# Seams between the phases of a four-layer scan network: an add moved into the Mamba passes, a norm interleaved with convolutions, weights loaded beside other phases

## The chip, the core and the metric

The kernel runs on one core of one Trainium2 chip. The metric is the device time of one execution in microseconds (us). Three executions of the kernel before gave 20165.96, 20166.1 and 20180.66 us, so its median is 20166.1 us.

## The reference

Four images of 48 x 48 positions and 192 channels (2304 tokens each) pass through four layers. Everything is float32. Cut to what matters here:

```python
# layer 0: two bidirectional Mamba blocks with a norm and a residual between them
def bimamba(u, i):              # P[i], P[i+1]: weights of the two directions
    return mamba(u, P[i]) + mamba(u[:, ::-1], P[i + 1])
...                             # first block on the columns of x (tokens w-major);
...                             # layernorm of its output, turned to rows, plus x: "mixed";
...                             # second block on "mixed": x1
# mamba(u): xz = u @ in.T; causal conv of 3 taps, silu; B, C, delta by projections;
#   h[t] = exp(delta[t] * A) * h[t-1] + delta[t] * u[t] * B[t];  y[t] = sum_n h[t] * C[t]
#   (y + xc * D) * silu(z) @ out.T            (384 inner channels, 16 states)
# layer 1 (VSS block), xl, xr = the two channel halves of x1
y = relu(bn2(conv3x3(bn1(xl), conv1))); y = relu(bn3(conv3x3(y, conv2)))
xl_out = relu(conv1x1(y, conv3))
xi, z = split(layernorm(xr) @ in_proj.T)      # 192 channels each
xi = silu(depthwise_conv3x3(xi))              # then four directional scans of xi,
...                                           # norm, gate silu(z), out projection, + x1
# layer 2 (SS2D): four directional scans, norm.  layer 3: row and column Mambas, MLP
```

Note that the two Mamba outputs of a block are added position by position. The kernel's second pass of a block runs its tokens backwards and writes its output in mirrored order (`mirror`), so both passes' outputs have the same layout in HBM.

## The kernel before, in words

**Phases.** `network` calls one function after the other: `mamba_pair` for weights 0 and 1 (0 to 3147 us of the profiled execution), `mix_images` (to 3330), `mamba_pair` for weights 2 and 3 (to 6483), `vss_inputs` (to 6997), `scan_layers` (layers 1 and 2, to 13478), `row_mambas` (to 19711) and `mlp`. The phases hand images to each other through HBM. Each opens its own pools of SBUF memory, so a tile of a later phase may have to wait until the tile of an earlier one whose memory it takes is free.

**Orders.** Each engine's instructions are kept in the order in which the program writes them: PE (matmuls), DVE (VectorE), ACT (ScalarE, `k.act`, `k.copy`), POOL (GpSimd, `k.g`), and SP, which issues all the DMAs (`nc.sync.dma_start`). An instruction that waits therefore holds back everything behind it on its engine. A tile pool with `bufs=n` gives out n buffers per tag; the next tile of that tag waits until the oldest is free.

**The scan.** A pass over an image is six `MambaJob`s of 384 tokens (`CH`), 48 jobs in a pair of passes over four images. A job has 12 groups: 3 blocks of 128 channels by 4 groups of 4 states. `run_jobs` walks over all groups. For each group DVE forms `inputs` (delta, u and the broadcast B, `bcb`) and runs the scan `h`; ACT forms the decays `a` two groups ahead; POOL copies the last state and multiplies `h` by C (`weigh`); PE sums over the states into `y` (`reduce`), one group behind. Once per block POOL also forms `dus` (delta times u, `drive`) and the gated `yt` (`gate`). The rest of a job's work (projections, convolution, gates, and the output projection of the job before) is given out as *units* with slots: a unit `((start, end), ...)` has its matmuls begun in one of the 12 groups and its result taken by ACT in another. The output projection of a job is made in slots 4 and 6 of the next job: two matmul units for the channel halves (`Q` = 96 each), taken to the tile `o` by ACT; with the second, SP stores `o` (288 KB). For B and C, SP issues four broadcasts (`bcb<-bc`) per job.

**The mix.** Before, the two passes of a pair write two image lists, `oa[0]` and `oa[1]`. `mix_images` loads for each image both outputs (`s0`, `s1`, 1728 KB each) and the residual `res`; POOL adds `s1` to `s0`, chunk by chunk (`both`, L903); then six norm stages follow, software-pipelined over 24 chunks: mean on PE, center on DVE (L173), square on ACT and its mean on PE, variance on DVE (L190), root on ACT, scale on DVE (L201), affine on ACT and DVE (L216). After an image's last chunk, `post` adds the turned result to `res`, one channel half on DVE and one on POOL (L907), and SP stores the image (`mixed`). Only then does the next `mamba_pair` load its weights (L796 to L870), derive `A` (ACT exp, DVE) and `diag` (DVE), and load the first `u`.

**The VSS inputs.** For each image `load` reads the two outputs of the second pair (`ob`), POOL adds them (L981), and the sum is stored as `x1`. `norm` normalizes the right channel half to `xn`. Per image the order is: the batch norm of the left half into the padded tile `pads[0]` (ACT), the projection of `xn` to two padded tiles (PE, ACT), 18 depthwise taps on DVE (L1026, L1030: 2 x 9 over a 96 x 2304 tile), the load of the next image, the first 3x3 convolution (PE, nine matmuls per chunk), the norm of the next image, the projection of `z` (PE, ACT), silu of `vxi` (ACT), its turned copy (POOL, L1057) and stores, then the second 3x3 convolution and the 1x1 convolution (PE, ACT) and the store of `xl`.

**The scan layers.** `scan_layers` first loads the weights of layers 1 and 2: per layer and direction `xpT`, `dtT` twice and `vec` (class `Weights`, L796 to L806), with `A` derived on ACT and DVE (L814), and `dsum` and `ddiag` on DVE; then the scan jobs of layer 1 begin by loading `xs` from the images `xi_hw` and `xi_wh`.

Of the kernel before, what the change touches and what calls it, by code (L numbers as in the profile page):

```python
# [17 lines left out]
B = 4  # L18
# [474 lines left out]
class MambaJob(ScanJob):  # L493
# [3 lines left out]

    skips = True

    def __init__(self, k, pools, w, c0, rev, prev, src, dst, mirror=False, twin=None):  # L500
        super().__init__(k, pools, w, c0, rev, prev)
        self.src, self.dst, self.mirror, self.twin = src, dst, mirror, twin
        self.paired = False
        if twin is not None:
            twin.paired = True
# [35 lines left out]
    def units(self, last):  # L541
# [41 lines left out]
        if self.twin is not None:  # L583
            self.z = self.twin.z
            outputs = last.outputs((7, 7), (9, 9)) if last is not None else []
            bc, deltas = self.projections(lambda: self.xs, (3, 3), (5, 5))
            return [conv(0, 0, 0), conv(1, 1, 2), conv(2, 2, 2), bc, *deltas, *outputs]
        outputs = last.outputs((4, 4), (6, 6)) if last is not None else []
# [8 lines left out]
            *outputs[1:],  # L597
            *deltas,
            gate(0, 9, 10),
# [17 lines left out]
    def outputs(self, *slots):  # L617
# [4 lines left out]
        jobs = [self] if self.twin is None else [self.twin, self]  # L622

        def project(m, slots):
            def act(ps):
                if m == 0:
                    self.o = k.tile(self.pools.one, [Q, 2, CH], "o")
                k.copy(self.o[:, m, ::step], ps)
                if m == 1:
                    d0 = L - CH - self.c0 if self.mirror else self.c0  # L630
                    k.nc.sync.dma_start(halves(self.dst)[:, :, d0 : d0 + CH], self.o)
# [15 lines left out]
        return [project(m, slots[m]) for m in range(2)]  # L647
# [65 lines left out]
def run_jobs(jobs, side=None):  # L713
# [29 lines left out]
    for t in range(len(groups) + gated):  # L743
# [8 lines left out]
        if at == taken + 3 and n + 1 == len(jobs) and n:  # L752
            Stream(jobs[n - 1].outputs((0, 0), (0, 0))).run(per)
# [28 lines left out]
    Stream(jobs[-1].outputs((0, 0), (0, 0))).run(per)  # L782
# [3 lines left out]
class Weights:  # L786


    def __init__(self, k, pool, wide, rank, xpT, dtT, vec, tag):
# [22 lines left out]
        self.A = k.tile(pool, [128, 3, n], f"A{tag}")  # L812
        k.act(self.A, self.vec[:, :, 1 : 1 + n], AF.Exp)
        nc.vector.tensor_scalar(self.A, self.A, -1.0, None, ALU.mult)  # L814


class MambaWeights(Weights):
    def __init__(self, k, pool, inT, xpT, dtT, vec, tag):
        super().__init__(k, pool, 128, 12, xpT, dtT, vec, tag)
        nc = k.nc  # L820
# [22 lines left out]
def mamba_pass(k, pools, w, rev, src, dst, mirror=False):  # L843
    jobs = []
    for n in range(NCH):
        c0 = (NCH - 1 - n if rev else n) * CH
        prev = jobs[-1] if jobs else None
        jobs.append(MambaJob(k, pools, w, c0, rev, prev, src, dst, mirror))
    return jobs
# [12 lines left out]
def mamba_pair(k, weights, srcs, outs, mirror):  # L862

    with ExitStack() as ctx:
        pool = ctx.enter_context(k.tc.tile_pool(name="w", bufs=1))
        ws = []
        for n, (inT, xpT, dtT, vec, outT) in enumerate(weights):
            w = MambaWeights(k, pool, inT, xpT, dtT, vec, f"_{n}")
            w.outT = k.tile(pool, [128, 3, C], f"outT_{n}")
            k.nc.sync.dma_start(w.outT, outT.rearrange("(k p) m -> p k m", p=128))  # L870
            ws.append(w)
        pools = ScanPools(k, ctx, 1, False)
        jobs = []
        for b in range(B):
            for n in range(2):
                jobs += mamba_pass(k, pools, ws[n], n == 1, srcs[b], outs[n][b], mirror and n == 1)
# [3 lines left out]
def mix_images(k, o, hw, norm, out_hw):  # L880


    nc, tc = k.nc, k.tc
    with (
# [5 lines left out]
        nc.sync.dma_start(nw, norm.rearrange("(k p) v -> p k v", p=Q))  # L890
        s0, s1, res = {}, {}, {}

        def pre(b):
            s0[b] = k.tile(pool, [Q, 2, L], "s0")
            nc.sync.dma_start(s0[b], halves(o[0][b]))
            s1[b] = k.tile(pool, [Q, 2, L], "s1")
            nc.sync.dma_start(s1[b], halves(o[1][b]))
# [3 lines left out]
        def both(b, c):  # L901
            at = slice(c * CH, (c + 1) * CH)
            nc.gpsimd.tensor_tensor(s0[b][:, :, at], s0[b][:, :, at], s1[b][:, :, at], ALU.add)  # L903

        def post(b):
# [7 lines left out]
            nc.sync.dma_start(halves(out_hw[b]), res[b])  # L913
# [7 lines left out]
        pipelined([both, *stages], pre, post)  # L921


def vss_inputs(k, o, bn, vec, conv1, conv2, conv3, inT, x1, xl, xi_hw, xi_wh, zs):
# [4 lines left out]
    with (  # L929
# [19 lines left out]
        w1 = k.tile(one, [Q, 9, Q], "w1")  # L949
        nc.sync.dma_start(w1, conv1.rearrange("t i o -> i t o"))  # L950
        w2 = k.tile(one, [Q, 9, Q], "w2")
        nc.sync.dma_start(w2, conv2.rearrange("t i o -> i t o"))
        w3 = k.tile(one, [Q, Q], "w3")
        nc.sync.dma_start(w3, conv3)
        win = k.tile(one, [Q, 4 * Q], "win")
        nc.sync.dma_start(win, inT)
        v = k.tile(one, [Q, 2, 10], "v")
        nc.sync.dma_start(v, vec.rearrange("(k p) v -> p k v", p=Q))
# [15 lines left out]
        x, xn = {}, {}  # L974

        def load(b):
            x[b] = k.tile(pool, [Q, 2, L], "vx")
            nc.sync.dma_start(x[b], halves(o[0][b]))
            x2 = k.tile(one, [Q, 2, L], "vx2")
            nc.sync.dma_start(x2, halves(o[1][b]))  # L980
            nc.gpsimd.tensor_tensor(x[b], x[b], x2, ALU.add)  # L981
            nc.sync.dma_start(halves(x1[b]), x[b])
            xn[b] = k.tile(pool, [Q, 1, L], "xn")

        def norm(b):
            stages = norm_stages(
# [10 lines left out]
            for t in range(NCH + len(stages) - 1):  # L997
# [4 lines left out]
        load(0)  # L1002
        norm(0)
        for b in range(B):
# [6 lines left out]
            )  # L1011
            for c in range(NCH):
                for e in range(2):
                    p, shaped = ps()
                    k.mm(
                        p, [(win[:, e * Q : (e + 1) * Q], xn[b][:, 0, c * CH : (c + 1) * CH])]
                    )
                    k.copy(inside(pads[2 + e], c), shaped)

            xi = k.tile(one, [Q, 2, L], "vxi")  # L1020
            for i in range(2):
                acc = square(xi[:, i, :])
                for t in range(9):
                    taps = pads[2 + i][:, t // 3 : t // 3 + S, t % 3 : t % 3 + S]
                    if t == 0:
                        nc.vector.tensor_scalar(  # L1026
                            acc, taps, v[:, i, 1:2], v[:, i, 0:1], ALU.mult, ALU.add
                        )
                    else:
                        nc.vector.scalar_tensor_tensor(  # L1030
                            acc, taps, v[:, i, 1 + t : 2 + t], acc, ALU.mult, ALU.add
                        )
            if b + 1 < B:
                load(b + 1)
            xlt = k.tile(one, [Q, L], "xlt")
            for c in range(NCH):
                _, shaped = ps()
                k.mm(shaped, [(w1[:, t, :], window(pads[0], c, t)) for t in range(9)])
                k.act(
                    inside(pads[1], c), shaped, AF.Relu, scale=scale[:, 1:2], bias=shift[:, 1:2]  # L1040
                )
            if b + 1 < B:
                norm(b + 1)
            z = k.tile(one, [Q, 2, L], "vz")
            for c in range(NCH):
                at = slice(c * CH, (c + 1) * CH)
                for e in range(2):
                    p, _ = ps()
                    k.mm(p, [(win[:, (2 + e) * Q : (3 + e) * Q], xn[b][:, 0, at])])
                    k.act(z[:, e, at], p, AF.Silu)  # L1050
            nc.sync.dma_start(halves(zs[b]), z)
            for i in range(2):
                k.act(xi[:, i, :], xi[:, i, :], AF.Silu)
            nc.sync.dma_start(halves(xi_hw[b]), xi)
            xiT = k.tile(one, [Q, 2, L], "vxiT")
            for i in range(2):
                nc.gpsimd.tensor_copy(square(xiT[:, i, :]), flipped(xi[:, i, :]))  # L1057
            nc.sync.dma_start(halves(xi_wh[b]), xiT)
            last = None
            for c in range(NCH + 1):  # L1060
                y = None
                if c < NCH:
                    p, shaped = ps()
                    k.mm(shaped, [(w2[:, t, :], window(pads[1], c, t)) for t in range(9)])
                    y = k.tile(pool, [Q, CH], "vy")
                    k.act(y, p, AF.Relu, scale=scale[:, 2:3], bias=shift[:, 2:3])
                if last is not None:
                    p, _ = ps()
                    k.mm(p, [(w3, last)])
                    k.act(xlt[:, (c - 1) * CH : c * CH], p, AF.Relu, bias=b3)  # L1070
                last = y
            nc.sync.dma_start(xl[b], xlt)
# [90 lines left out]
def scan_layers(k, layers, ends):  # L1163
# [3 lines left out]
    with ExitStack() as ctx:  # L1167
        nc = k.nc
        pool = ctx.enter_context(k.tc.tile_pool(name="w", bufs=1))
# [7 lines left out]
        for n, (xpT, dtT, vec, rank, post, src) in enumerate(layers):  # L1177
            ws = [
                Weights(k, pool, 64, rank, xpT[i], dtT[i], vec[i], f"_{n}{i}") for i in range(4)
            ]  # L1180

            ds = k.tile(pool, [64, 3, 6], f"ds{n}")
            nc.sync.dma_start(ds, post.rearrange("(k p) v -> p k v", p=64))
            dsum = k.tile(pool, [64, 3], f"dsum{n}")
# [458 lines left out]
```

## Time and profile before

| | |
|---|---|
| median of 3 executions | 20166.1 us |
| profiled execution, its own time | 20169.74 us |
| span of the profile | 20168.0 us, mean PE clock 0.933 |
| busy: PE, DVE, ACT, POOL | 87%, 90%, 63%, 73% |
| chain that ended last, by engine | POOL 39%, DVE 33%, issue 12%, PE 10%, DMA 2%, ACT 2% |

The page gives busy time of each engine, the same in 40 slices of the span, the DMA queues, the chain of work that ended last (followed back from the last instruction, at each step to what released it), and the costliest groups of instructions: line, engine, operation, output and inputs with shapes, count, then busy time and mean ns of one, then the engine's idle time just before and what ended most of it. A line number such as L56 can be that of a helper through which many operations are issued; the names of the tiles tell them apart. The trace answers further questions: the busy time in chosen windows, what each engine waited for, and the chain in order of time ("SPq" is SP issuing; "issue" is time in which the engine waited for nothing that the profile shows).

### The profile page before, as it was taken

To read this page: it belongs to the slowest core of one execution; us is meant where nothing else is said; L and a number is where in the kernel's file an instruction comes from. 1 tells how busy PE (TensorE), PEld (TensorE's weight loads), DVE (VectorE), ACT (ScalarE), POOL (GpSimd) and SP (SyncE) were. 2 spreads that over 40 slices of the span, in tenths; PEclk is the share of its full clock that TensorE was granted. 3 is DMA by queue.
4 is the path that set the end of the run, shared out by engine and by line. 5 is a ranking of instruction groups with operands and counts; after the bars stand their busy time and mean duration, and the time that the engine had idled before them with its cause. 6 is when DMAs were issued, how large, how long until landed. Compare 5 with 4: busy or idle time off the path is not lost.

```text
span 20168.0 us, 159086 instructions
## 1 busy us (share of the span) xinstructions
PE 17562.1 (87%) x48144; PEld 8299.8 (41%) x48144; DVE 18228.9 (90%) x7435; ACT 12794.8 (63%) x22448; POOL 14681.1 (73%) x10748
## 2 busy tenths in 40 slices
PE   8999996999997778888888888879999988989988
PEld 4444443444444322233333333334444444444444
DVE  8999997999998499999999999969999989999993
ACT  6666664666665366666666766656666656666663
POOL 7777775777777177878877878757777767777770
PEclk9999998999999889989999999989999999999999
DMA  3323334332333266666666666642222222222222
GB/s 115 108 104 109 108 110 116 111 110 104 108 107 110 74 129 141 139 148 147 140 147 143 139 141 135 144 112 106 106 106 106 103 94 104 102 105 106 104 103 59
DMA packets 476472, 2320.46 MB, mean 115 GB/s; under 512 B 74552, under 2 KB 313760, under 8 KB 315104
## 3 DMA queue, kind: packets, MB, share of 16 engines
q1 hardware_dynamic: 475616, 2310.29, 40.5%
q8 instruction: 386, 6.32, 0.1%
q14 instruction: 470, 3.85, 0.1%
HBM read 2110.68 MB, written 199.40 MB: 115 GB/s over the span
## 4 chain that ended last, share of the span: by engine, by line
POOL 39%; DVE 33%; issue 12%; PE 10%; DMA 2%; ACT 2%; SPq 0%; DVEq 0%; POOLq 0%; ACTq 0%
POOL h L56 31%; DVE h L56 21%; DVE inputs L56 11%; PE y L56 4%; POOL dus L56 3%; PE ps L56 3%; POOL state L56 2%; POOL yt L56 1%; PE vps L114 1%; POOL bcb L56 1%; PE mop L114 1%; PE mps L114 1%; DMA bcb<-bc 1%; DVE vxi L1030 1%; ACT a L93 1%
## 5 line engine op out<-in xcount | busy, mean ns | idle before, releaser
L56 POOL TENSOR_TENSOR h<-h,bcb 128x1536 f32<-128x1536 f32 x3456 | 11908.1, 3446 | 1763.4 <-DVE h L56 1489.6
L56 DVE TENSOR_TENSOR_SCAN h<-a,inputs 128x1540 f32<-128x1540 f32 (+1 forms) x3456 | 11609.0, 3359 | 447.9 <-ACT a L93 11.7
L93 ACT ACTIVATE a<-delta,A 128x384 f32<-128x384 f32 (+1 forms) x13824 | 7432.0, 602 | 3399.6 <-DVE h L56 3388.4
L56 PE MATMUL y<-h,ident 128*128 128x384 f32 x18432 | 6807.0, 518 | 583.2 <-POOL h L56 578.1
L56 DVE TENSOR_TENSOR inputs<-du,bcb 128x1540 f32<-128x1540 f32 (+1 forms) x3456 | 6114.9, 1769 | 555.2 <-ACT du L93 164.1
L56 PEld LDWEIGHTS y<-h,ident 128*128 128x128 f32 x18432 | 3630.4, 201 | 3615.6 <-POOL h L56 1091.8
L56 PE MATMUL y<-h,sum 128*64 128x384 f32 x9216 | 3672.6, 548 | 600.1 <-POOL h L56 492.7
L56 PEld LDWEIGHTS y<-h,sum 128*64 128x64 f32 x9216 | 1295.0, 150 | 2927.8 <-issue 1739.8
L56 POOL COPY state<-h 128x4 f32<-128x4 f32 x2304 | 431.6, 187 | 2388.4 <-DVE h L56 2364.8
L56 PE MATMUL ps<-xh,diag 128*128 128x384 f32 x4032 | 1419.2, 492 | 194.6 <-ACT xc L93 194.5
L56 PE MATMUL ps<-u,inT 96*128 96x384 f32 x3456 | 1262.2, 497 | 200.3 <-ACT z L93 134.6
L56 PE MATMUL ps<-bcd,dtT 12*128 12x384 f32 (+1 forms) x2304 | 1019.6, 550 | 388.5 <-ACT delta L93 384.5
L56 PEld LDWEIGHTS ps<-xh,diag 128*128 128x128 f32 x4032 | 752.4, 189 | 787.3 <-ACT xc L93 281.5
L93 ACT ACT_TABLE_LOAD x793 | 1017.4, 1283 | 14.0
L90 ACT ACT_TABLE_LOAD x785 | 1007.2, 1283 | 14.3 <-PEq L1633 0.7
L56 PEld LDWEIGHTS ps<-u,inT 96*128 96x128 f32 x3456 | 652.7, 192 | 711.9 <-ACT z L93 212.5
L93 ACT ACTIVATE delta<-ps,vec 128x384 f32<-128x384 f32 x1152 | 631.4, 578 | 322.1 <-PE ps L56 315.0
L56 PE MATMUL ps<-yt,outT 128*96 128x384 f32 x2304 | 789.6, 486 | 0.7 <-POOL yt L56 0.7
L56 PEld LDWEIGHTS ps<-bcd,dtT 12*128 12x128 f32 (+1 forms) x2304 | 383.7, 192 | 957.1 <-ACT delta L93 621.9
L56 POOL TENSOR_TENSOR dus<-delta,xc 128x384 f32<-128x384 f32 x576 | 574.9, 998 | 139.6 <-ACT delta L93 139.6
L93 ACT ACTIVATE du<-dus 128x384 f32<-128x384 f32 x1152 | 558.1, 484 | 160.0 <-DVE inputs L56 154.0
L56 POOL TENSOR_TENSOR dus<-delta,xs 128x384 f32<-128x384 f32 x576 | 574.1, 997 | 59.8 <-ACT delta L93 59.8
(132 smaller groups left out, 9285.9 us busy)
## 6 DMA issues: line engine op xcount, KB each, us to landing
bcb<-bc SPq DMA_DIRECT2D x384, 1540.0 KB
bcb<-bc SPq DMA_DIRECT2D x768, 770.0 KB
bcb<-bc SPq DMA_DIRECT2D x384, 1536.0 KB
y<-o SPq DMA_DIRECT2D x192, 288.0 KB
xs<-xi_wh SPq DMA_DIRECT2D x96, 288.0 KB
xs<-xi_hw SPq DMA_DIRECT2D x96, 288.0 KB
added<-y SPq DMA_DIRECT2D x96, 288.0 KB
xs<-x_wh SPq DMA_DIRECT2D x96, 288.0 KB
```

The costliest lines, as they stand in the source:

```text
L56: return lambda *a, **kw: self.tc.keep_in_program_order(op(*a, **kw))
L90: self.in_order(self.nc.scalar.preload_act_table_set(LOG_EXP))
L93: return self.in_order(self.nc.scalar.activation(out, in_, func, **kw))
L114: (engine or self.nc.tensor).matmul(out, lhsT, rhs, start=start and i == 0, stop=stop and i == n - 1)
L1030: nc.vector.scalar_tensor_tensor(acc, taps, v[:, i, 1 + t : 2 + t], acc, ALU.mult, ALU.add)
```

## The change

Four things are changed; the scan layers' jobs, the row Mambas and the MLP are as before.

First, in layer 0 the second pass of a pair gets the first one's output as `prior`. Each of its jobs loads the matching 288 KB of it when its output units are made; POOL adds the two channel halves to `o` in slots 7 and 8 (the units behind the projections' slots 4 and 6), and the store of `o` is issued after the second add. The first pass writes to `first`; the second writes the sum, to `oa` in the first pair and straight to `x1` in the second.

Second, `mix_images` loads one image in place of two, without the adds of L903. The first image comes in two parts (first chunk, the rest); an image is fetched one image ahead; the result is stored in channel halves, each after its own add. The weights of the second pair are loaded and derived within the mix, when image 1 begins.

Third, `vss_inputs` reads `x1` in channel halves, right half first, and has no add. The norm of the next image is written step by step between the chunks of the first convolution and the depthwise taps; the batch norm of the next image's left half follows the taps, before `z`. Silu, turned copy and stores of `vxi` are made by channel halves, between chunks 2 and 4 of the second convolution.

Fourth, the weights of the scan layers are loaded after image 0 of `vss_inputs` and derived after image 1 (`beside`), in a pool that is opened around both functions.

```diff
 class MambaJob(ScanJob):
-        outputs = last.outputs((4, 4), (6, 6)) if last is not None else []
+        outputs = last.outputs((4, 4), (6, 6), (7, 7), (8, 8)) if last is not None else []
...
+        def store():
+            k.nc.sync.dma_start(halves(self.dst)[:, :, d0 : d0 + CH], self.o)
+
+        def add(m):
+            k.g.tensor_tensor(self.o[:, m, :], self.o[:, m, :], prior[:, m, :], ALU.add)
+            if m == 1:
+                store()
...
+        units = [project(m, slots[m]) for m in range(2)]
+        if self.prior is not None:
+            prior = k.tile(self.pools.one, [Q, 2, CH], "prior")
+            k.nc.sync.dma_start(prior, halves(self.prior)[:, :, d0 : d0 + CH])
+            units += [(slots[2 + m], lambda: None, lambda m=m: add(m)) for m in range(2)]
+        return units
...
 def mamba_pair(k, weights, srcs, first, outs, ahead=None):
+        if ahead is None:
+            load()
+        else:
+            ahead(load)
...
+            jobs += mamba_pass(k, pools, ws[0], False, srcs[b], first[b])
+            jobs += mamba_pass(k, pools, ws[1], True, srcs[b], outs[b], True, first[b])
...
 def mix_images(k, o, hw, norm, out_hw, load):
+        def fetch(b):
             s0[b] = k.tile(pool, [Q, 2, L], "s0")
-            nc.sync.dma_start(s0[b], halves(o[0][b]))
+            for n in range(2 if b == 0 else 1):
+                at = slice(0, L) if b else (slice(0, CH), slice(CH, L))[n]
+                nc.sync.dma_start(s0[b][:, :, at], halves(o[b])[:, :, at])
...
             res[b] = k.tile(pool, [Q, 2, L], "res")
             nc.sync.dma_start(res[b], halves(hw[b]))
-        def both(b, c):
-            at = slice(c * CH, (c + 1) * CH)
-            nc.gpsimd.tensor_tensor(s0[b][:, :, at], s0[b][:, :, at], s1[b][:, :, at], ALU.add)
+        def pre(b):
+            if b + 1 < B:
+                fetch(b + 1)
+            if b == 1:
+                load()
...
-            nc.sync.dma_start(halves(out_hw[b]), res[b])
+                nc.sync.dma_start(out_hw[b][m * Q : (m + 1) * Q, :], res[b][:, m, :])
...
-        pipelined([both, *stages], pre, post)
+        fetch(0)
+        pipelined(stages, pre, post)
...
 def vss_inputs(k, x1, bn, vec, conv1, conv2, conv3, inT, xl, xi_hw, xi_wh, zs, beside):
+        def load(b):
+            x[b] = k.tile(pool, [Q, 2, L], "vx")
+            for m in (1, 0):
+                nc.sync.dma_start(x[b][:, m, :], x1[b][m * Q : (m + 1) * Q, :])
...
-            nc.gpsimd.tensor_tensor(x[b], x[b], x2, ALU.add)
-            nc.sync.dma_start(halves(x1[b]), x[b])
...
+            step = norm(b + 1) if b + 1 < B else lambda t: None
+            for t in range(NCH + 6):
+                if t < NCH:
+                    first_conv(t)
+                step(t)
+                for n in range(18):
+                    if n * 2 // 3 == t:
+                        depthwise(b, n)
+            if b + 1 < B:
+                pad_first(b + 1)
             z = k.tile(one, [Q, 2, L], "vz")
...
+                y = second_conv(c) if c < NCH else None
+                if c in (2, 4):
+                    inner(b, c // 2 - 1)
                 if last is not None:
+                    third_conv(b, c - 1, last)
                 last = y
+            beside(b)
...
+            def beside(b):
+                if b == 0:
+                    for n, rank in ((1, 6), (2, 12)):
+                        of = (d[f"L{n}_{v}"] for v in ("xpT", "dtT", "dir"))
+                        weights.append(LayerWeights(k, pool, n, *of, rank, d[f"L{n}_post"]))
+                if b == 1:
+                    for w in weights:
+                        w.derive(k)
```

`LayerWeights` holds what `scan_layers` loaded at its start: the `Weights` of four directions with `ds`, and a method `derive` for `A`, `dsum` and `ddiag`.

## Prediction

> **What bounds the kernel now.** I read the page first (busy shares, costliest groups), then a table of windows for the seams between phases, then for each seam the waits and the chain that ended last. Times are us from the start of the span.
>
> ```profile
> L56 POOL TENSOR_TENSOR h<-h,bcb 128x1536 f32<-128x1536 f32 x3456 | 11908.1, 3446 | 1763.4 <-DVE h L56 1489.6
> L56 DVE TENSOR_TENSOR_SCAN h<-a,inputs 128x1540 f32<-128x1540 f32 (+1 forms) x3456 | 11609.0, 3359 | 447.9 <-ACT a L93 11.7
> L56 DVE TENSOR_TENSOR inputs<-du,bcb 128x1540 f32<-128x1540 f32 (+1 forms) x3456 | 6114.9, 1769 | 555.2 <-ACT du L93 164.1
> ```
>
> Each of the 3456 scan groups costs DVE 1.77 + 3.36 us and POOL 3.45 us: DVE sets the pace in the scans. The change leaves those groups alone, so what matters is the seams, where the windows show no engine full:
>
> ```profile
> 3147.00:3330.00 183.00, 81.25 (x192) 36.37 (x192) 100.08 (x100) 58.83 (x96) 71.15 (x28) 0.71 0.63 152
> 6483.00:6997.00 514.00, 416.97 (x1200) 201.44 (x1200) 235.97 (x150) 170.58 (x284) 110.92 (x16) 0.89 0.30 87
> 6997.00:7110.00 113.00, 43.16 (x89) 14.49 (x90) 46.45 (x41) 38.38 (x74) 32.83 (x29) 0.60 0.44 87
> ```
>
> (Busy time of PE, PEld, DVE, ACT, POOL; PE clock; DMA share; GB/s.) In the mix DVE works 100 of 183 us; in the VSS inputs PE works 417 of 514; while the weights of the scan layers load, nothing does much. The chain names what was waited for, first in the mix:
>
> ```profile
> 3151.20 41.70 DMA s<-oa
> 3193.04 1.81 POOL s L903
> ...
> 3320.19 6.02 POOL res L907
> 3326.23 7.86 DMA mixed<-res
> ...
> 3348.69 13.81 PE ps L56 x36
> ```
>
> Two whole images and a residual must land before the first add, 41.7 us. At the end the last POOL half, its store, the weights of the second pair and one u tile follow in series. Then the VSS inputs:
>
> ```profile
> 6490.94 11.36 DMA vx<-ob
> 6502.44 9.89 POOL vx L981
> ...
> 6528.60 9.98 DVE ln_xm L201
> ...
> 6552.73 40.47 DVE vxi L1030 x16
> ...
> 6616.55 45.68 PE vps L114 x132
> ...
> 6993.22 4.55 DMA xl<-xlt
> ...
> 7041.45 4.04 DMA xs<-xi_wh
> ```
>
> Per image DVE's depthwise taps (L1026, L1030) run, then the next image's norm, and only then the z projection and the second convolution on PE. Between xl's store and the first xs stand 43.5 us of weight loads (64 SP issues of about 0.65 us).
>
> **The change part by part.** *The add moves into the scan.* Gone: 24 POOL adds in the mix (L903, 1.81 us) and 4 in the VSS inputs (L981). New: 96 POOL adds of o and prior, 96x384, and 48 loads of prior, 288 KB, in the reverse jobs. No such add is in the trace; the nearest row is POOL's 128x384 product (dus, 0.998 us), so at most 96 x 1.0 = 96 us, at least 0. The schedule puts them behind h in slots 7 and 8 of a job's 12, where POOL has nothing else:
>
> ```profile
> 3079.60 3.44 POOL h L56
> 3083.04 0.96 POOL dus L56
> 3083.99 0.13 POOL bcb L56
> 3084.13 0.54 issue
> 3084.95 3.44 POOL h L56
> ```
>
> A slot that holds such a product (dus) still takes 5.35 us from h to h, and POOL still idles 0.54 us; plain slots take 5.36 us and idle 1.5. So I take 0, hidden by DVE's 5.13 us; without that cover it is 1.0 us each. The o store now waits for the second add. Behind it on SP stand the prior load and two bcb fetches; those two were issued no earlier than the h of slot 9 before, one slot later, so I take 0. The prior load adds 1.3 us at 222 GB/s to a queue that the page shows about a third busy. After each pair's last job the add is exposed: 1 us.
>
> *The mix.* It reads one sum instead of two images (7.1 MB less). The DMA rate in the full stretch 3180–3193 is 222 GB/s. After the last store (2.5 us, issued 1.0 later) the first chunk lands at about 3154.7 (a 288 KB load: 4.04 us), against 3192.9 for the whole image. DVE's own work is 100.1 us, less about 6 that L903 stretched L201, plus two weight sets (A and diag, 2.7 us each in the trace) = 99.5. But SP is in order: inT_0, s0 and res of images 0 and 1, s0 of image 2 and outT_0 stand ahead of vec_1: 9.7 MB / 0.222 = 43.8 us from 3150.7, landing at 3196.5. ACT's Exp of A_1 waits for it and all of ACT's norm work queues behind; DVE dries up near 3174 with 17.7 us done. Then 81.8 more, 8 for the last chunk's way through ACT (3308 to 3316 before), 6.0 for the POOL half: 3292.5. Store 7.86, SP 0.45, u 5.70: first matmul at 3306.5 instead of 3348.7, as the weights are there already. Gain 42. Bounds: without the stall 62; with twice the stall and no earlier weights (about 22 and 3) 17.
>
> The Trainium skill, "DMA: Bandwidth & Descriptors", section Bandwidth, measures 341 GB/s for a 1 MB load. By that figure the 9.7 MB take 28.5 us, the stall shrinks by 15 and this gain would be 57; the row of this case shows 222, so the sum does not use it.
>
> *VSS inputs, head.* x1 of image 0 is in HBM before the scan ends, so neither the 11.36 load nor the 9.89 add is on the path; what is late next is bnt, which waits for the last store (5.78, 1.0 later: 6484.1) and lands near 6488.5. ACT's first square comes near 6489 instead of 6514.6: 25.6 earlier. L201's 9.98 us (0.55 undisturbed; POOL's next add ran beside it) goes as well: 9. Depthwise starts at 6515.3 instead of 6549.9: gain 34.6.
>
> *VSS inputs, per image.* From depthwise to depthwise it takes 122.7, 123.3 and 115.2 now. DVE's norm ops (6 x 3 x 0.55 = 9.9) are put between the taps; DVE remains the limit up to z: 43.3 + 9.9, then xn 0.7, the pad 2.3 and a table load 1.3. From the first tap to z that is 57.5, less what overlaps: about 57, instead of 66.7, 68.5 and, undisturbed, 58.5. The second half was 56.0 and 54.8; the pad (2.3) leaves it and the SILUs (2 x 2.1) enter it: 56.6. So 113.6 per image; 117.5 for image 1, where ACT loads a table and derives A before the projection. Gains 9.1, 5.8 and 1.6: 16.5. Bounds: -10 (if PE, dry for 16 us, restarts slowly: the clock was 0.71 in the mix) to 30.
>
> *Weights.* The 64 loads move behind image 0's convolutions. There SP's 41.6 us stand ahead of the x load of image 2, which is needed some 80 us later: hidden. A and dsum come after image 1. The 43.5 us go, since xs follows xl's store directly: bounds 30 to 43.5.
>
> Sum: 42.2 + 34.6 + 16.5 + 43.5 = 136.8. The profiled execution took 20169.7 (span 20168.0), 3.6 above the median of 20166.1. A profiled run should then take about 20033 and the median 20029, which I put at 20030. Within 0.2% (40 us) no difference can be told.
>
> **Rivals.** *The mix does not stall and the images overlap more* (DMAs do not come in the order of issue, or PE gets ahead): 20 more in the mix and up to 13 in the images: 20000 to 20010. For: PE idles 16 us per image in my account. Against: the full DMA row.
>
> *The seams give half*: the mix 17, images -10, the rest as above, less 10 for weights: 75, so 20090. For: POOL and DVE stretch each other at these seams (L201 2.5 to 10 us for 0.55 to 0.95); the new res halves meet too.
>
> *POOL's adds are not hidden*: each delays the next h by 1.0: 96 back, 20126, within 0.2%. Against: the dus slots above.
>
> *Slower: SP's queue.* The o store, which now waits for the last POOL add, holds back the bcb fetches behind it, and DVE stands still in each of 48 reverse jobs. The price is 48 us per us of stall: 2.8 us eat the whole gain, and from 3.7 us it is slower by 0.2%. One group period, 5.36 us, gives +257 - 137 = +120: 20286. For: the fetches are 1.5 MB, 7.1 us at 222 GB/s, and a missed slot costs whole microseconds. Against: they are issued some 28 us ahead of need, so the stall must first eat 14 us or more.
>
> **How the numbers follow.** Forecast 0.60 (20005–20060), no stall and more overlap 0.14 (20000–20010), half the gain 0.14 (20060–20095), adds exposed 0.07 (20126), slower 0.05 (20286). The likeliest gives 20030. With the two neighbouring cases the range from 19992 to 20092 holds about 0.85 by this count, and I take it as 0.8 for what I have not seen. Faster by over 0.2% means below 20126: 0.60 + 0.14 + 0.14 = 0.88; same 0.07; slower 0.05.
>
> **What would show it.** Right: reverse-job periods still 5.3–5.4 us; first mix matmul near 3155, ACT waiting for vec about 20 us, first scan matmul near 3306; depthwise starts about 113 us apart; no SP train between xl and xs. Wrong: DVE's idle time before `inputs` put down to DMA bcb in reverse jobs; a scan stage longer than 3153 us; L201 or L1030 stretched beside a POOL add.

## The result, and the profile after

The changed kernel takes 20034.0 us (median of 4 runs, 20029.1 to 20039.8) against 20170.2 us for the kernel before (4 runs, 20166.0 to 20180.7). The ratio is 0.9932 with a 95% interval of 0.9915 to 0.9949: 136 us faster. The forecast was 20030 us.

Both profiles can be cut at the same marks: the issue of the last o store of each pair, the first matmul of the second pair, the first depthwise tap of each image, the store of xl, and the first load of xs. Between these marks the order of work is fixed, so they tell more than the total.

| stage, us | before | after | gain | foreseen |
|---|---|---|---|---|
| first pair, to its last o store | 3146.7 | 3147.5 | -0.8 | 0 (tail -1) |
| mix, to the first matmul of the second pair | 202.0 | 154.8 | 47.2 | 42.2 (tail included) |
| second pair, to its last o store | 3128.6 | 3132.9 | -4.2 | 0 (tail -1) |
| head of the VSS inputs, to the first tap | 72.5 | 37.2 | 35.4 | 34.6 (tail included) |
| images 0, 1, 2 (first tap to first tap) | 122.7, 123.3, 115.1 | 113.9, 114.2, 111.9 | 20.9 | 16.5 |
| image 3, to the store of xl | 82.4 | 82.4 | 0.0 | 0 |
| xl to the first xs | 48.2 | 6.4 | 41.8 | 43.5 |
| from there to the end of the span | 13126.5 | 13127.2 | -0.7 | 0 |

The gains add up to 139.6 us, the difference of the two spans (20168.0 and 20028.4).

The page shows the scan groups as they were; only the seams moved:

```profile
L56 POOL TENSOR_TENSOR h<-h,bcb 128x1536 f32<-128x1536 f32 x3456 | 11914.0, 3447 | 1764.2 <-DVE h L56 1489.3
L56 DVE TENSOR_TENSOR inputs<-du,bcb 128x1540 f32<-128x1540 f32 (+1 forms) x3456 | 6115.4, 1770 | 561.0 <-ACT du L93 205.9
```

The windows of the three seams, with the same columns as before:

```profile
3142.00:3299.00 157.00, 84.73 (x203) 37.99 (x201) 99.14 (x127) 59.44 (x100) 40.91 (x9) 0.72 0.60 150
6436.00:6895.00 459.00, 411.99 (x1200) 199.41 (x1198) 213.58 (x166) 170.42 (x291) 41.54 (x12) 0.92 0.24 67
6895.00:6970.00 75.00, 41.75 (x87) 14.06 (x88) 43.92 (x25) 36.99 (x67) 33.19 (x29) 0.68 0.62 141
```

The mix has the same DVE work in 157 us instead of 183, and is still not full. In the VSS inputs POOL falls from 111 to 42 us.

In this profile the chain of waits breaks off at 6461 us, so its shares by engine are not comparable with those of before. For the mix the timelines serve. ACT (start, length, what, and in brackets the idle time before it with what ended it), then PE:

```profile
3176.27 0.23 ACT L93 ACTIVATE A<-vec 128x48 f32<-128x48 f32 x1
3194.47 0.24 ACT L93 ACTIVATE A<-vec 128x48 f32<-128x48 f32 x1 [17.97 <-DMA vec<-in_L_vec]
```

```profile
3302.27 7.20 PE L56 MATMUL ps<-u,inT 96*128 96x384 f32 x12 [25.05 <-DMA u<-mixed]
```

ACT stands 18.0 us at the second A, where some 20 were foreseen, and the second pair's first matmul comes at 3302.3. In the VSS inputs the chain does reach back:

```profile
6475.20 17.70 DVE vxi L1056 x7
6492.90 0.47 DVE ln_rs L190
6493.37 0.46 DVE ln_xm L173
6493.83 7.59 DVE vxi L1056 x3
...
6528.76 1.28 ACT L93
6530.06 0.49 ACT vz L93
6530.60 46.25 PE vps L114 x132
...
6894.79 6.28 DMA xl<-xlt
```

The norm's DVE steps stand between the taps, and z starts at 6530.6, 58 us after the first tap (6472.3).

### The profile page after: what moved, and what is told of

It is laid out like the page before. It is cut to its first block, busy times and chain, and to the rows that moved or that the text cites. A ratio compares the mean times of both kernels' runs of the same rounds, so it can differ in the third digit from the quotient of the medians.

```text
span 20028.4 us, 159197 instructions
## 1 busy us (share of the span) xinstructions
PE 17551.3 (88%) x48144; PEld 8281.4 (41%) x48144; DVE 18198.7 (91%) x7435; ACT 12796.7 (64%) x22447; POOL 14681.9 (73%) x10816
## 4 chain that ended last, share of the span: by engine, by line
DVE 35%; POOL 13%; PE 10%; issue 5%; ACT 2%; DMA 2%; DVEq 0%; SPq 0%; POOLq 0%; ACTq 0%
DVE h L56 23%; DVE inputs L56 12%; POOL h L56 10%; PE y L56 5%; PE ps L56 3%; POOL dus L56 1%; PE vps L114 1%; ACT a L93 1%; PE mop L114 1%; PE mps L114 1%; DMA bcb<-bc 1%; POOL state L56 1%; DVE vxi L1056 1%; DVEq L56 0%; POOL bcb L56 0%
## 5 line engine op out<-in xcount | busy, mean ns | idle before, releaser
L93 ACT ACTIVATE o<-ps 96x384 f32<-96x384 f32 x288 | 140.3, 487 | 716.6 <-PE ps L56 716.6
```

The costliest lines, as they stand in the source:

```text
L93: return self.in_order(self.nc.scalar.activation(out, in_, func, **kw))
```

## The experiments

Each kernel is the changed one with the edit shown. The code from the first xs to the end is the same in all of them, and took 13124.2 to 13145.7 us in their profiles. So totals that differ by less than about 20 us say nothing here, and each edit is read from its stage. A stage scatters too where nothing in it was changed: over the kernels that leave it alone the first pair took 3145.9 to 3149.6 us, the mix 154.6 to 158.2, the second pair 3131.3 to 3132.9, and the three images together 337.0 to 340.1.

**e1: no add.**

```diff
-            jobs += mamba_pass(k, pools, ws[1], True, srcs[b], outs[b], True, first[b])
+            jobs += mamba_pass(k, pools, ws[1], True, srcs[b], outs[b], True)
```

> Left out: the adds of the first pass's output in the scans, with their loads of prior; the second pass stores its own output alone, right after ACT has taken it. What the 96 adds, the 48 loads and the later store cost is read as the difference to the changed kernel. Theory (hidden behind DVE, as the two scan stages of the changed kernel suggest, whose last h starts 1.4 and 1.8 us later than before, plus 1 us of tail each): 4 to 6 us faster than the changed kernel. Rival (each add delays the next h by its 1.0 us): 90 to 100 us faster. Rival (the store's wait on SP holds back the bcb fetches): DVE's idle time before inputs, put down to DMA, falls by more than 10 us.

The first pair took 3146.1 us (after: 3147.5), the second 3131.4 (3132.9): 1.3 and 1.4 us less. That lies within what kernels with the adds take, so no price can be read from it; what a trace shows of the adds' cost is the last one of each pair, 1.0 us long, ahead of the last store. The rest was hidden: in the stretches looked at (300 to 3100 and 3400 to 6400 us) DVE's waits before `inputs` are the same with and without the adds, but for a single one of 1.6 us, and none is put down to a DMA. The whole time (20038.7 us, 20035.4 to 20049.5) shows no gain. The two rivals fall. Of the 4.2 us that the second pair lost against before, some 3 are there without the adds as well and remain without an explanation (1.3 of it lies between the first matmul and the first h).

**e2: each add twice.**

```diff
             k.g.tensor_tensor(self.o[:, m, :], self.o[:, m, :], prior[:, m, :], ALU.add)
+            k.g.tensor_tensor(self.o[:, m, :], self.o[:, m, :], prior[:, m, :], ALU.add)
```

> Every POOL add of prior is done twice (so the output holds the first pass's part twice): 2.0 us in slots in which POOL idles 1.5. Theory (DVE sets the pace and POOL may lag, since h has four buffers and POOL has 1.5 us over in the slots after it): 2 to 10 us slower than the changed kernel. Rival 1 (the idle time of that slot is all there is): 0.5 us in each of 96 slots, 48 us slower. Rival 2 (POOL is the bound in these jobs): 96 us slower.

The time is 20081.8 us (20072.4 to 20088.2), 48 us over the changed kernel's median; in the profiles the two pairs take 19.9 and 21.4 us more, 41.3 in all or 0.43 us for each of the 96 slots. My theory fell and rival 1 is close. The waits of DVE from 300 to 3100 us in this run show how:

```profile
DVE inputs L56 <- POOL bcb L56: 21.8, 38, 0.6
```

and POOL's timeline in two such slots:

```profile
2936.87 2.06 POOL L56 TENSOR_TENSOR o<-o,prior 96x384 f32<-96x384 f32 x2
2938.88 0.18 POOL L56 COPY bcb<-state 128x4 f32<-128x4 f32 x1
2939.01 0.18 POOL L56 COPY state<-h 128x4 f32<-128x4 f32 x1
2939.27 3.45 POOL L56 TENSOR_TENSOR h<-h,bcb 128x1536 f32<-128x1536 f32 x1
```

In the changed kernel this wait is not among DVE's in that window. After its h and adds POOL copies the state into the next `bcb` (`carry`), and DVE's next `inputs` needs that copy. So POOL can't fall behind from one slot to the next: what it does beyond its 1.5 us of idle time in a slot delays DVE in the same slot, at most 0.6 us at a time here.

**e3: the scan layers' weights written behind the last image.**

```diff
-                if b == 0:
+                if b == B - 1:
                     for n, rank in ((1, 6), (2, 12)):
...
-                if b == 1:
+                if b == B - 1:
                     for w in weights:
```

> The weights of the scan layers are loaded and derived after the last image of the VSS inputs, as before, all else as changed. Theory (64 issues of 0.65 us on SP between the store of xl and the first xs): 41 to 44 us slower than the changed kernel, all of it between those two. Rival (they were partly hidden, or their move delays an x load, so that taking them back there helps the images): under 30 us slower.

Neither: from xl to xs it took 6.4 us, as in the changed kernel. SP's timeline shows that the loads did not move:

```profile
6447.19 0.74 SPq L814 DMA_DIRECT2D xpT<-in_L_xpT  x1
...
6500.63 0.61 SPq L1230 DMA_DIRECT2D ds<-in_L_post  x1
```

SP issues them from 6447 us (in the changed kernel from 6443), around the first tap of image 0 at 6475.8, although they are written behind image 3. So the description of the kernel is wrong where it has every engine keep the program's order: by the code only what goes through ACT's helpers and `k.v`, `k.g`, `k.t` does. Plain DMAs (here) and `nc.vector` instructions (e7 below) are placed when the kernel is built.

**e9: the pool of these weights opened after the VSS inputs.**

```diff
+        vss_inputs(
+            k, x1, *(d[f"L1_{v}"] for v in ("bn", "conv", "conv1", "conv2", "conv3", "inT")),
+            xl, *xi, zs, lambda b: None,
+        )
         with tc.tile_pool(name="w", bufs=1) as pool:
-            weights = []
-
-            def beside(b):
-                if b == 0:
...
+            for n, rank in ((1, 6), (2, 12)):
+                of = (d[f"L{n}_{v}"] for v in ("xpT", "dtT", "dir"))
+                weights.append(LayerWeights(k, pool, n, *of, rank, d[f"L{n}_post"]))
+            for w in weights:
+                w.derive(k)
```

> The pool of the scan layers' weights is opened only after the VSS inputs are done, and the loads and derivations follow it; all else as changed. In e3 only the place in the program was moved back, and the loads were still issued during image 0 (from 6447 to 6501 us). Theory (what lets the loads go early is that their memory is free, not where they are written): the 64 issues come back between the store of xl and the first xs, which lie 40 to 50 us apart again in place of 6.4. Rival (SP's queue has room for them anyway): under 20 us.

From xl to xs it took 49.5 us again, and the time was 20084.8 us (20080.0 to 20090.3). SP from xl on:

```profile
6892.27 0.30 SPq L1083 DMA_DIRECT2D xl<-xlt  x1
6898.66 0.75 SPq L814 DMA_DIRECT2D xpT<-in_L_xpT  x1
...
6939.01 0.61 SPq L1230 DMA_DIRECT2D ds<-in_L_post  x1
...
6941.78 2.56 SPq L463 DMA_DIRECT2D xs<-xi_wh  x4
```

The theory holds: it is the pool that lets the loads go early. In e9 SP waits 5.8 us at the first of them for xl's store to land; with the pool opened around both functions they wait for nothing of the VSS inputs' end. For these loads the place in the program does nothing.

**e4: the norm in one piece behind the taps.**

```diff
-            for t in range(NCH + 6):
-                if t < NCH:
-                    first_conv(t)
-                step(t)
-                for n in range(18):
-                    if n * 2 // 3 == t:
-                        depthwise(b, n)
+            for n in range(18):
+                depthwise(b, n)
+            for c in range(NCH):
+                first_conv(c)
+            for t in range(NCH + 6):
+                step(t)
```

> The norm of the next image stands in one piece after the 18 taps and the first convolution again; the add stays in the scan and the x loads stay early. The changed kernel gained 20.9 us from the first tap to the last store of xl. Theory (most of it is the POOL add beside the taps that is gone, which had stretched taps and L201 in two of the images: they took 122.7 and 123.3 where the undisturbed one took 115.2): about 10 us slower than the changed kernel, 3.4 per image, the norm's round trips through PE and ACT, which the taps no longer cover. Rival (the interleaving is what gained): about 20 us slower, 7 per image.

The three images took 115.5, 116.7 and 115.1 us (after: 113.9, 114.2, 111.9), 7.2 us more together, and DVE's timeline has the 18 taps in one piece. So the interleaving is worth 7.2 us; the other 13.7 of the 20.9 stayed with the interleaving undone, which leaves what else was changed there: no POOL add, loads that come early, the batch norm ahead of z, and `vxi` by halves. The kernel before tells which: its image 2, with no POOL add beside it, took 115.1 us, close to e4's images, and its images 0 and 1, with one each, took 7.6 and 8.2 more. POOL and DVE in its image 1:

```profile
6677.44 10.27 POOL L981 TENSOR_TENSOR vx<-vx,vx 96x4608 f32<-96x4608 f32 x1 [41.84 <-DMA vx<-ob]
```

```profile
6675.32 50.22 DVE L1030 SCALAR_TENSOR_TENSOR vxi<-pad,v,vxi 96x2304 f32<-96x2304 f32 x16
```

The 16 taps took 50.2 us beside the add, and 40.5 in the two other images (in image 0 it is a step of the norm that is stretched, L201, 5.73 us for 0.55). That fits the theory, with 2.4 instead of 3.4 us per image for the interleaving.

**e5: the weights of the second pair written behind the mix; e6: their small loads ahead of it.** In e6, `load` is split: the constructor (xpT, dtT, vec) runs before the mix, and `decays`, the diagonals, inT and outT stay where image 1 begins.

```diff
-            if b == 1:
-                load()
...
         pipelined(stages, pre, post)
+        load()
```

> The weights of the second pair are loaded and derived behind the mix in the program, no longer when image 1 begins. In the changed kernel ACT stands 18.0 us at the Exp of A_1 for its vec, DVE 14.1 us. Theory (the stall in the middle is real cost, and the loads find room in the queue before the last store anyway): the first matmul of the second pair comes 10 to 17 us earlier than in the changed kernel. Rival (loading them beside the mix is what gains there): it comes about 15 us later, the 14.6 us that stood between the last store and the first matmul before, beyond u.

> The small loads of both weight sets (xpT, dtT, vec) are issued ahead of the images of the mix, the large ones (inT, outT) stay where they are. Theory (vec_1 waits in the queue behind 9.7 MB of images): ACT's wait at A_1 goes from 18.0 us to under 2 and the first matmul of the second pair comes 12 to 17 us earlier. Rival (the images' own arrival holds up the norm then: image 1 lands when the stall ends): under 5 us earlier, with PE waiting for s instead.

The mix took 138.5 us in e5 and 143.7 in e6, against 154.8: 16.3 and 11.1 less. In e5 the first matmul:

```profile
3286.73 6.43 PE L56 MATMUL ps<-u,inT 96*128 96x384 f32 x12 [25.32 <-DMA u<-mixed]
```

Both theories hold (e6 a microsecond short of its range), and ACT no longer waits for vec at A. The stall was real cost on the path. The whole times (20028.2, 20026.4 and, for e8 below, 20031.9 us) fall by less than the stages and lie within the 20 us above. Whether loading beside the mix gains anything e5 does not tell, as the loads stayed there: SP issued the first set's small weights and inT at 3147 to 3151 us, much as in the changed kernel, outT and the second set at 3229 to 3260 instead of 3179 to 3193, and none behind the last store at 3275. So here the line `if b == 1` did move loads, and it decides when ACT comes to the two Exp (3264.8 us in e5).

**e8: both halves of the residual add on DVE.**

```diff
-                (nc.vector, nc.gpsimd)[m].tensor_tensor(
+                nc.vector.tensor_tensor(
```

> In the mix both halves of the residual add are done by DVE; POOL has none. In the changed kernel POOL's half takes 6.2 us alone and 10 to 11 behind DVE's, and one DVE instruction beside it takes 5.0 to 6.3 us in place of 0.5 to 0.95 (three times). Theory (POOL's half holds up DVE about 5 us each, which is more than DVE's own 4.05): 3 to 6 us faster than the changed kernel, POOL's 10 at the end of the last image becoming 8. Rival (the two halves do run side by side, and DVE now has 16 us more): 8 to 12 us slower.

The mix took 147.2 us, 7.6 less, somewhat more than the theory had. In the changed kernel POOL's half looks like this:

```profile
3205.43 6.20 POOL L940 TENSOR_TENSOR res<-res,s 96x2304 f32<-96x2304 f32 x1 [58.00 <-PE ln_ps L114]
3232.60 10.89 POOL L940 TENSOR_TENSOR res<-res,s 96x2304 f32<-96x2304 f32 x1 [20.96 <-DVE s L216]
```

and on DVE, beside and after it:

```profile
3232.44 4.13 DVE L940 TENSOR_TENSOR res<-res,s 96x2304 f32<-96x2304 f32 x1
...
3238.67 5.03 DVE L216 TENSOR_SCALAR s<-ln_xm,nw 96x384 f32<-96x384 f32 x1
```

POOL's 10.9 us are 4.1 behind DVE's half and some 6 of its own, in which a DVE instruction of 0.47 us takes 5.0. By these lengths the halves do not run side by side, and DVE's own 4.1 us are cheaper than POOL's 6.2.

**e7 and e10: the taps later.** One tap per step of the norm, the rest behind it and behind the batch norm of the next image; in e10 the taps and the norm's steps are issued through `k.v`, which keeps their order.

```diff
                 step(t)
-                for n in range(18):
-                    if n * 2 // 3 == t:
-                        depthwise(b, n)
+                if b + 1 < B:
+                    depthwise(b, t)
             if b + 1 < B:
                 pad_first(b + 1)
+            for n in range(12 if b + 1 < B else 0, 18):
+                depthwise(b, n)
```

> In the VSS inputs one tap is placed in each of the 12 norm steps and the last six taps behind the norm and the batch norm of the next image, so that z and the second convolution need not wait for them. Theory (PE, dry for some 15 us per image in front of z, works through; the taps still end before the SILUs of the second half need them): 7 to 10 us less per image in three images, 20 to 30 us faster than the changed kernel. Rival (the SILUs and the next projection wait for the late taps, and the time is lost again there): under 6 us.

> As e7 (one tap in each step of the norm, the rest of the taps after it), but now DVE keeps the order in which taps and norm steps are written; in e7 DVE ran them in nearly the same order as in the changed kernel, and the image intervals were the same to 0.1 us. Theory (z waits for the end of the norm, which now comes 15 to 20 us earlier, while the taps end in time for the SILUs): 7 to 10 us less in each of three images. Rival 1 (DVE in a fixed order waits for PE's means between the taps, and the SILUs and the next projection come later): no gain or a loss in each image.

In e7 the images took the same as in the changed kernel to 0.02 us: DVE's timeline has taps and norm in the same order as there, so the edit had no effect. In e10 they took 114.4, 116.2 and 115.1 us, 5.7 more in all: rival 1. PE and then DVE show what the norm waits for:

```profile
6475.59 18.87 PE L114 MATMUL vps<-pad,w 96*96 96x384 f32 x58
6494.34 0.89 PE L114 MATMUL ln_ps<-ln_sq,mean 96*96 96x384 f32 x2
```

```profile
6495.27 0.55 DVE L56 TENSOR_SCALAR ln_rs<-ln_ps 96x384 f32<-96x384 f32 x1 [4.80 <-PE ln_ps L114]
```

The next image's means stand in PE's order behind the first chunks of the first convolution. From the first tap to the SILU of z, the changed kernel and then e10 (columns as in the windows of the seams):

```profile
6472.33:6530.06 57.73, 48.75 (x141) 22.72 (x139) 53.06 (x44) 20.12 (x34) 0.00 (x0) 0.89 0.20 38
6475.61:6535.21 59.60, 47.77 (x141) 22.25 (x139) 37.80 (x37) 20.12 (x33) 0.00 (x0) 0.90 0.19 36
```

In the changed kernel DVE is busy for 53 of the 58 us, so it does look like the limit; with 15 us less on DVE z comes no earlier. Room on DVE alone does not help, as the way through PE and ACT takes as long. e10 also fixes DVE's order, and what that alone costs was not run.

**e11: e5, e8 and e10 together.**

> The changed kernel with three edits: the weights of the second pair written behind the mix (e5: the mix 16.3 us shorter), both residual halves on DVE (e8: 7.6 shorter), and the ordered late taps of e10. Theory (the first two are parts of the same chain, the norm's DVE work in the mix, and add up but for a few us; the third is apart): mix 18 to 24 us and images 20 to 30 us shorter, 38 to 54 us in all. Rival (the stall that e5 removed covers what e8 saves): mix 16 us shorter, as in e5 alone.

The mix took 129.9 us: 24.9 less, e5's and e8's parts added up (16.3 + 7.6 = 23.9). The images were 7 us slower, as e10 lets expect. The time was 20020.7 us (20017.3 to 20027.8).

**e12: e5 and e8, and z ahead of the norm.**

```diff
+            z = k.tile(one, [Q, 2, L], "vz")
+            for e in range(2):
+                for c in range(NCH):
+                    p, _ = project(b, c, 2 + e)
+                    k.act(z[:, e, c * CH : (c + 1) * CH], p, AF.Silu)
+            nc.sync.dma_start(halves(zs[b]), z)
             step = norm(b + 1) if b + 1 < B else lambda t: None
...
             if b + 1 < B:
                 pad_first(b + 1)
-            z = k.tile(one, [Q, 2, L], "vz")
...
```

> The changed kernel with the weights of the second pair written behind the mix and both residual halves on DVE (as in e11, where the mix took 129.9 us against 154.8), the taps as in the changed kernel, and the projection of z with its SILU moved ahead of the first convolution and of the norm of the next image. In the changed kernel PE waits 8 to 15 us in front of z, behind ACT's end of that norm; e10 showed that the taps are not what holds it. Theory (z needs only this image's norm; with it out of the way PE runs on into the second convolution, and an image of about 103 us of matmuls takes 104 to 108 us): three image intervals 5 to 9 us shorter each, the mix 130, together 38 to 50 us shorter than the changed kernel. Rival (ACT's order then holds the second convolution's ReLUs behind that same norm, and PE's four psum tiles fill): intervals within 2 us of the changed kernel's, 25 us in all from the mix alone.

The images took 96.4, 98.0 and 96.2 us, 49.5 less in all, more than the theory's 15 to 27, which took PE's 103 us per image as given; the mix 129.4. The time is 19967.8 us (4 runs, 19966.0 to 19971.5), against 20170.0 for the kernel before on the same chip: a ratio of 0.9900, with an interval of 0.9883 to 0.9916. It beats both kernels. PE in front of z in the changed kernel:

```profile
6530.60 8.82 PE L114 MATMUL vps<-xn,win 96*96 96x384 f32 x16 [5.86 <-ACT vz L93]
```

and in e12, in the stretch in which the changed kernel runs dry:

```profile
6493.93 0.81 PE L114 MATMUL ln_ps<-ln_sq,mean 96*96 96x384 f32 x2
6494.58 1.45 PE L114 MATMUL vps<-pad,w 96*96 96x384 f32 x4
6495.87 0.81 PE L114 MATMUL ln_ps<-ln_sq,mean 96*96 96x384 f32 x2
6496.51 7.26 PE L114 MATMUL vps<-pad,w 96*96 96x384 f32 x22
```

No idle time stands in brackets, and none does in the rows around them. The windows of the three images, in the changed kernel and in e12, and that of all of e12's VSS inputs add the second part:

```profile
6472.33:6812.43 340.10, 308.08 (x898) 148.85 (x897) 156.90 (x123) 129.30 (x220) 24.71 (x6) 0.92 0.23 66
6442.82:6733.43 290.61, 290.30 (x898) 144.89 (x897) 158.33 (x123) 133.81 (x224) 24.64 (x6) 1.00 0.27 78
6416.00:6840.00 424.00, 404.28 (x1214) 198.21 (x1214) 213.70 (x171) 182.12 (x307) 38.40 (x16) 0.96 0.28 78
```

Over the three images PE stood still for 32.0 us and now for 0.3, and the same number of matmuls kept it busy for 308.1 us and now for 290.3, at a clock of 1.00 instead of 0.92: the two differences are the 49.5 us. An image now takes PE's own time, so PE is the limit there.

## Why the prediction was right, point by point

**The total.** 136.8 us were foreseen, and 139.6 came in the two profiles and 136 in the medians. That this is so close is in part luck: by stage the difference is +4.2 in the mix, -0.2 in the head, +4.4 in the images, -1.7 at the weights and -3.2 in the second pair beyond its tail, and the part of the kernel that no edit touches scatters by 20 us.

**The scans.** 0 was right for the adds, loads and later stores: by e1 they cost no more than a few us in all, 2 of them the two ends. That the second pair lost some 3 us besides was not foreseen. The reason given was too loose: what covers an add is the 1.5 us for which POOL idles in the slot that DVE's 5.13 us set, and e2 shows the price beyond it, 0.43 us per slot for two adds that exceed it by about 0.5. The slower rival (SP's queue) left no trace: nothing of DVE's idle time in these jobs is put down to a DMA. That a store held up for several microseconds would be dear was not tried.

**The mix.** 42.2 was foreseen for mix and tail, 47.2 - 0.8 = 46.4 came. The order of loads held: vec_1 was there at 3194.4 (foreseen 3196.5), and from 3152 us to then the DMA engines were full at 231 GB/s, near the row's 222. The 341 GB/s that the Trainium skill's "DMA: Bandwidth & Descriptors", section Bandwidth, gives for a 1 MB load over 128 partitions was not reached. What the account left out is that SP itself stood still: it issued s0 of image 2 only at 3178.2, when DVE had centered the last chunk of image 0 and its buffer was free, and vec_1 behind it from 3180.1. The term that was mis-sized is the stall: 18.0 us for ACT and 14.1 for DVE, where I had DVE dry for 22. From POOL's end to the first matmul it took 11.5 us instead of 14.0, and the last POOL half 10.0 instead of 6.0, for the reason that e8 shows.

**The head.** 34.6 foreseen for head and tail, 35.4 - 1.0 for the tail of the second pair came; both waits (vx, POOL's add) are gone.

**The images.** 113.6, 117.5 and 113.6 foreseen; 113.9, 114.2 and 111.9 came. Image 1 pays nothing visible for deriving A. Most of the gain is the missing POOL add, as the prediction had it with its undisturbed image; to the interleaving it gave 1.6 us per image (115.2 to 113.6), and e4 measures 2.4. From the first tap to z 57 us were foreseen, and 57.7, 57.1 and 56.6 came. But the account "DVE remains the limit up to z" is only half of the cause: DVE is nearly full there, yet by e10 z comes no earlier with less on DVE, and by e12 what cost the time is that z stands behind the end of the next image's norm at all. That PE's idle time also lowers its clock was named as a risk and given no term; e12 puts it at 17.8 us over three images.

**The weights.** 43.5 foreseen, 41.8 came; xl's store took 6.3 us rather than 4.6. The number was right and the reason given, their new place behind image 0, was not: e3 and e9 show that it is the pool.

## What to carry to other kernels

Before crediting a new place in the program, find out what decides the order: here a pool opened earlier was worth 42 us, and moving the line that writes the loads moved none of them (e3), while in the mix it did (e5). SP's timeline tells which it is. An engine off the critical path hides work only as far as its idle time before the next hand-over; read that from the slot, not from its share of the span. Where an engine that should be full waits in front of an instruction, ask whether that instruction needs what stands ahead of it in the order: moving z, which needed nothing of the next image's norm, was worth more than everything that was interleaved.

## What the runs showed of the hardware that was not expected

Two DMA issues on SP took 7.45 and 3.53 us in the mix of the changed kernel, where nearly all of its 3350 take 0.3 to 0.9 us and no other more than 2.6, at a time when whole images were queued:

```profile
3180.49 7.45 SPq L824 DMA_DIRECT2D vec<-in_L_vec  x1
3187.98 0.95 SPq L828 DMA_DIRECT2D vec<-in_L_vec  x1
3188.97 3.53 SPq L852 DMA_DIRECT2D inT<-in_L_inT  x1
```

An issue can itself be held up, and with it all that stands behind it on SP; what it waits for these runs do not tell. And idle time on PE cost more than its length: with about the same matmuls in the VSS inputs, PE was busy 417 us at a granted clock of 0.89 (before), 412 at 0.92 (after) and 404 at 0.96 (e12), the less it stood still the better. Behind an idle time of 5.86 us the 16 matmuls of z in the changed kernel took 8.82 us; 33 of the same shape without one took 10.85 in e12:

```profile
6439.78 10.85 PE L114 MATMUL vps<-xn,win 96*96 96x384 f32 x33
```
